# A second Strassen-Winograd level on one block product of seven, row statistics from sums, and a new emission order

## The chip, the cores and the metric

The kernel runs on one core of a Trainium2 chip, in fp32 throughout. The metric is the device time of one launch in microseconds, as the median over repeated runs. Besides the runs there is one execution recorded by the hardware profiler. Its rows name TensorE as PE (with PEld for its weight loads), VectorE as DVE, ScalarE as ACT, GpSimd as POOL and SyncE, which issues most DMAs, as SP.

## The reference

The input `x` is 128 batch entries of 128 nodes by 512 features, `adj` a 128 by 128 matrix. Four layers follow, each `x = layernorm(x + layer(x))` over the 512 features:

```
layer 0:  (adj x) W0 + bias
layer 1:  q = x Wq^T, k = x Wk^T, v = x Wv^T; rel = adj^T * (q k^T), each row divided by its norm; rel v
layer 2:  h = x W; s1, s2 = h a1, h a2; e = leaky_relu(s1 + s2^T) * adj; elu(softmax(e) h + beta h)
layer 3:  max over nodes of relu(...), with adj as both weights
```

The kernel uses that layer 1's `q k^T` is `(x M) x^T` with `M = Wq^T Wk`, that layer 2's `softmax(e) h + beta h` is `((softmax(e) + beta I) x) W`, and that layer 3's maximum collapses to `relu(max(adj x) + b)`, one value per row, which is added to the row of `x`.

## The kernel before

**Tiling.** Four batch entries form a group, and there are 32 groups (`G = 4`, `NG = 32`). A group passes through four products of 512 by 512 by 512: `y` (layer 0, times `W0`), `m` (layer 1, times `M`), `v` (layer 1, times `Wv`) and `z` (layer 2, times `W`). Around them stand smaller TensorE pieces for each batch entry: aggregates `p_y` (`adj x`, transposed), scores `p_rel`, attends `p_o`, gathers `p_z` and widens `p_a` (layer 3).

**One product.** `product` (L350) does each of the four with one Strassen-Winograd level: seven block products of 256 by 256 by 256 in place of eight. One block product is four matmuls with 256 moving columns (`by_rows` L324, `by_columns` L337). In the profile an fp32 matmul is two instructions, so a block product is a row of eight. The left factors are sums of blocks of the transposed activations, made on GpSimd (`left_factors` L305). The right factors are sums of weight blocks, made once on VectorE (`weight_blocks` L157). The block products run in the order 1, 2, 6, 5, 7, 3, 4. They are accumulated in three PSUM regions: products 1, 6, 7 and 4 in one bank (tag `r0`, two buffers), and product 2, then 5 and 3, in another (tag `r12`, one buffer). After each product the region is read out (`out`, L380), by a ScalarE copy or a VectorE add, and the next product into that region has to wait for this read.

**PSUM.** The eight banks are `r0` twice, `r12` once, `wa` (two banks that hold constant rows for the dots) and three of tag `ps` (`bank`, L85), which all the smaller pieces take in turn.

**Statistics.** Every layernorm takes `bn_stats` and `bn_aggr` on VectorE (`stats`, L397), a small VectorE operation and a power on GpSimd (`spread` in `norm`, L408), a small VectorE operation (`shift`) and an apply per batch entry on ScalarE. In layer 1, `residual` (L590) makes the new row on VectorE and takes its statistics directly after it, and `dots` (L605) follows with two multiply-and-sum operations per entry. In layer 2, `exp` on ScalarE and `elu` (L807) on VectorE do the same for its output. Layer 3 takes its own sums: squares on ScalarE, a maximum on VectorE and, on ScalarE, an add of that maximum that also sums the row (`top`, L860). Its `spread` (L868) works on these sums.

**Order.** Each engine executes in program order, and the order of the program is written by hand. Every piece is emitted at a time from `TABLE` (L235), in units of which a group takes 28. `FIRST` and `LAST` override it for the first two and the last three groups. All pieces of all groups are sorted by their time, so that in one period of 28 units four groups are interleaved: `m` of one group, `y` of the next, `v` of the first again, `z` of the group before. A piece emits its instructions on all engines it uses at one point: an aggregate, for instance, is four matmuls and the ScalarE copy behind them. Transposes of `x` for layer 1, of `rel` and of `e` are made in 32 by 32 blocks on VectorE (`turn_blocks`, `turn_rel`, `turn_blocks_2`) and completed by DMAs from the SP queue (`move`, `move_rel`, `move_2`); so is the spreading of `s2`, which `leaky` (L690) reads. Groups 0 and 1 use TensorE transposes (`turn`, L500), as do the softmax weights of the last two groups (`turn_att`, L734).

Of the kernel before, what the change touches and what calls it, by code (L numbers as in the profile page):

```python
# [8 lines left out]
FP = mybir.dt.float32  # L9
# [4 lines left out]
EPS = 1e-5  # L14
# [15 lines left out]
def kernel(  # L30
# [54 lines left out]
    def bank(name):  # L85
        return psum.tile([P, D], FP, tag="ps", name=name, bufs=3)

# [31 lines left out]
    nc.sync.dma_start(w2_sb, w2.rearrange("(k p) f -> p k f", p=P))  # L119
    a_sb = data.tile([P, 2, D], FP, tag="x3", name="a_sb")  # L120
    nc.sync.dma_start(a_sb.rearrange("p s d -> p (s d)"), on_all(a2, 2 * D))
# [35 lines left out]
    def weight_blocks(at, key, w, keep=0, tag=None):  # L157

        def blk(kh, ch):
            return w[:, 2 * kh : 2 * kh + 2, H * ch : H * ch + H]

        t = {}

        def factor(i):
            if i == 0:
                home, args = (const, {}) if tag is None else (data, dict(tag=tag))
                u = home.tile([P, 3 + keep, 2, H], FP, name=f"t_{key}", **args)
                t.update({2: u[:, 0], 3: u[:, 1], 4: u[:, 2]})  # L170
                t[1] = u[:, 3] if keep else blk(0, 1)
                bw[key] = {
                    1: blk(0, 0), 2: blk(1, 0), 3: blk(1, 1), 4: t[4], 5: t[1], 6: t[2], 7: t[3],
                }
            to, left, op, right = (
                (3, blk(1, 1), ALU.subtract, blk(0, 1)),
                (2, t[3], ALU.add, blk(0, 0)),
                (4, blk(1, 0), ALU.subtract, t[2]),
                (1, blk(0, 1), ALU.subtract, blk(0, 0)),
            )[i]  # L180
            dve.tensor_tensor(t[to], left, right, op)

        for i in range(4):
            emit(at[i], factor, i)

    bw = {}

# [9 lines left out]
    def prepare_dots(k):  # L197

        for i in range(2):
            scr = work.tile([P, D], FP, tag="scr", name=f"scr_wa_{i}_{k}", bufs=2)  # L200
            dve.scalar_tensor_tensor(
                scr,
                w2_sb[:, k, :],
                1.0,
                a_sb[:, i, :],
                op0=ALU.mult,
                op1=ALU.mult,
                accum_out=col[:, i, k : k + 1],
            )
# [21 lines left out]
    def row(at, step, n=G):  # L231
        return [at + i * step for i in range(n)]


    TABLE = dict(  # L235
        load=[-20], y=row(0.5, 1), y_sums=row(4.3, 0.5), y_w=row(7, 1, 7),
        stats0=row(14.4, 0.4), norm0=[16.2], apply0=row(16.8, 0.33),
        turn=row(21.4, 1), turn_blocks=row(18.4, 0.6),
        move=row(20.5, 0.1), x_sums=row(25.3, 0.5), m=row(28, 1, 7), scores=row(36.5, 1),
        masked=[39.95], squares=[40.4], turn_rel=[40.3],  # L240
        move_rel=row(41.2, 0.1), inverse=[42.5], v=row(42, 1, 7), attend=row(50.6, 1),
        residual=row(51.0, 1), dots=[51.7, 53.8, 54.9, 55.6], norm1=[54.6], scale=[57.2],
        apply1=row(65.4, 0.33),
        spread=[57.3], leaky=[62.6], weighted=[62.9], greatest=[63.9], exps=[64.0],
        divide=[65.2], turn_att=[68.6], with_beta=[69.0], turn_blocks_2=[65.7], move_2=[65.8], gather=row(71.5, 1),
        z_sums=row(75.3, 0.5), z_w=row(77, 1, 7), exp=[86.0, 87.0, 96.0, 99.6],
        elu=[86.4, 87.4, 96.8, 100.3], norm2=[101.4], apply2=row(102.4, 0.33),
        widen=[104.2, 104.9, 105.6, 106.3], top=[104.7, 105.4, 106.1, 106.8],
        norm3=[107.4], apply3=row(108.4, 0.33), store=[109.8],
    )  # L250

    FIRST = {
        0: dict(stats0=row(15.8, 0.02), norm0=[15.95], apply0=row(18.0, 0.1), turn=row(20.4, 0.3),
                dots=row(57.8, 0.1), scale=[58.9], spread=[61.6]),
        1: dict(y=row(-9.5, 0.3), y_sums=row(-4.0, 0.1), apply0=row(18.0, 0.1), turn=row(20.3, 0.3),
                x_sums=row(22.5, 0.5)),
# [47 lines left out]

    def left_factors(at, s, aT, tag, name, keep):  # L305

# [14 lines left out]
        emit(at[2], lambda: pool.tensor_tensor(s["f"][7], blk(0, 0), blk(1, 0), ALU.subtract))  # L321
        emit(at[3], lambda: pool.tensor_tensor(s["f"][3], blk(0, 1), s["f"][6], ALU.subtract))

    def by_rows(p, a, b, first):  # L324
# [24 lines left out]

    def product(at, name, mul, s, w, c, fresh, begin=None, before=None, lead=0.7):  # L350

# [28 lines left out]
        def out(i):  # L380
# [3 lines left out]
            else:  # L384
                dve.tensor_tensor(dst, p, dst, ALU.add)

        for n, i in enumerate(ORDER):
            if before is not None and i in (1, 5):
                emit(at[n] - (0.7 if i == 5 else lead), fill, REGION[i])
            emit(at[n], step, i)  # L390
            emit(at[n] + 0.72, out, i)
# [11 lines left out]

    def norm(at, apply_at, s, g, t):

        n = G // len(at)

        def spread(i):  # L408
            sl = slice(i * n, i * n + n)
            ve = small.tile([P, n], FP, tag=f"ve{n}", name=f"ve_{g}_{i}")  # L410
            dve.tensor_scalar(ve, s["mv"][:, sl, 1], EPS, None, op0=ALU.add)
            s["r", i] = small.tile([P, n], FP, tag=f"rstd{n}", name=f"rstd_{g}_{i}")
            pool.tensor_tensor(s["r", i], ve, mhalf[:, sl], ALU.pow)
# [24 lines left out]
    def layer0(g, t):  # L438
        s = {}

        def aggregate(b):
# [13 lines left out]
            )  # L455

        if g > 0:
            emit(t["load"][0], load, g)
        each(t["y"], aggregate)
        left_factors(t["y_sums"], s, "yT", "s_yz", f"y_{g}", 0)  # L460
        product(
# [7 lines left out]
            before=bias_halves,  # L469
            lead=4.4 if g == 0 else 0.7,  # L470
        )
        each(t["stats0"], lambda b: stats(s, f"0_{g}", b, x1[g][:, b, :]))
# [3 lines left out]
    def layer1(g, t):  # L476
        s = {}


# [110 lines left out]
        def residual(b):  # L590
            if b == 0:
                x2[g] = data.tile([P, G, D], FP, tag="x2", name=f"x2_{g}")
            dve.scalar_tensor_tensor(
                x2[g][:, b, :],
                s["o", b],
                s["rn"][:, b : b + 1],
                x1[g][:, b, :],
                op0=ALU.mult,
                op1=ALU.add,
            )  # L600
            if g < NG - 1:
                stats(s, f"1_{g}", b, x2[g][:, b, :])


        def dots(b):  # L605
            if b == 0:
                s["d"] = small.tile([P, 2, G], FP, tag="d12", name=f"d12_{g}")
            for i in range(2):
                scr = work.tile([P, D], FP, tag="scr", name=f"scr_{g}_{b}_{i}", bufs=2)
                dve.scalar_tensor_tensor(  # L610
# [26 lines left out]
        else:  # L637
            each(t["turn_blocks"], turn_blocks)
            each(t["move"], move)
        left_factors(t["x_sums"], s, "xT", "s_x", f"x_{g}", 1)  # L640
        product(t["m"], f"m_{g}", by_columns, s, "m", middle_block, True, begin_middle)
        each(t["scores"], scores)
# [7 lines left out]
        emit(t["inverse"][0], inverse)  # L650
        product(t["v"], f"v_{g}", by_rows, s, "v", rows_of(lambda: s["v"]), True, begin_values)
        each(t["attend"], attend)
# [4 lines left out]
        emit(t["scale"][0], scale_dots)  # L657
        norm(t["norm1"], t["apply1"], s, f"1_{g}", lambda: x2[g])

# [5 lines left out]
    def layer2(g, t):  # L665
        s = {}
        late = g >= NG - 2


# [64 lines left out]
        def turn_att(i):  # L734
            if i == 0:
                s["p"] = bank(f"p_eT_{g}")
            for b in range(i * n, i * n + n):
                pe.transpose(s["p"][:, b * P : (b + 1) * P], s["e"][:, b, :], ident)

        def with_beta(i):  # L740
            if i == 0:
                s["eT"] = work.tile([P, G, P], FP, tag="eT", name=f"eT_{g}")
            dve.tensor_tensor(
                s["eT"][:, i * n : i * n + n, :],
                s["p"].rearrange("p (b n) -> p b n", b=G)[:, i * n : i * n + n, :],
                beta_b[:, i * n : i * n + n, :],
# [60 lines left out]
        def elu(b):  # L807
            if b == 0:
                if g < NG - 1:
                    x3[g] = data.tile([P, G, D], FP, tag="x3", name=f"x3_{g}")  # L810
                else:
                    x3[g] = work.tile([P, G, D], FP, tag="xB", name=f"x3_{g}")
# [3 lines left out]
            )  # L816
            dve.scalar_tensor_tensor(x, s["m", b], 1.0, x, op0=ALU.min, op1=ALU.add)
            stats(s, f"2_{g}", b, x)

# [14 lines left out]
        if g < NG - 1:  # L834
            left_factors(t["z_sums"], s, "zT", "s_yz", f"z_{g}", 0)
            product(t["z_w"], f"z_{g}", by_rows, s, "2", rows_of(lambda: s["c"]), True, begin)
        else:
            each(t["z_w"], direct)
        each(t["exp"], exp)
        each(t["elu"], elu)  # L840
        norm(t["norm2"], t["apply2"], s, f"2_{g}", lambda: x3[g])

    def layer3(g, t):
        s = {}

        def widen(b):
            s["a", b] = bank(f"p_a_{g}_{b}")
            pe.matmul(s["a", b], adjT, x3[g][:, b, :], start=True, stop=True)  # L850
# [155 lines left out]
```

## Time and profile before

| What | Value |
|---|---|
| time, median of 3 runs | 2174.16 us (2173.9 to 2174.24) |
| the profiled execution, its time | 2173.83 us |
| its span, first to last instruction | 2172.0 us |
| mean granted TensorE clock | 0.996 |
| TensorE busy | 2149.1 us, 99% |
| VectorE busy | 1560.6 us, 72% |
| ScalarE busy | 1115.4 us, 51% |
| GpSimd busy | 720.8 us, 33% |
| DMA queue of SP | 135.22 MB, 24.8% of 16 engines |

Busy time is the time in which an engine had an instruction in it. TensorE's instructions overlap, so its pace is read from the starts of consecutive instructions and not from their durations. The span is what the rows cover; the execution's time is 1.83 us longer. "Idle before" in a row is what the engine stood still ahead of that group, with the releaser behind an arrow. Line L26 stands in nearly all rows, because one helper records every instruction; the names of the tiles tell the rows apart.

### The profile page before, as it was taken

What the parts mean: (1) busy time and instruction counts of PE and PEld (TensorE: products, weight loads), DVE (VectorE), ACT (ScalarE), POOL (GpSimd) and SP (SyncE); (2) the same over time, 40 slices, a digit from 0 to 9 for tenths busy, and PEclk for the clock granted to TensorE, in tenths of its full rate; (3) what the DMA queues carried; (4) which work ended last, traced back from release to release, by engine and by line L of the source; (5) the groups of instructions that cost most, each with busy time, mean ns of one, the idle gap of its engine ahead of it and who ended that gap; (6) DMA issues with size and microseconds to landing.
All of it is one profiled execution on the core that took longest, in us unless ns stands there. A gap on an engine that the chain in (4) does not pass through costs nothing.

```text
span 2172.0 us, 31973 instructions
## 1 busy us (share of the span) xinstructions
PE 2149.1 (99%) x10887; PEld 1820.3 (84%) x10887; DVE 1560.6 (72%) x3429; ACT 1115.4 (51%) x2470; POOL 720.8 (33%) x589
## 2 busy tenths in 40 slices
PE   9999999999999999999999999999999999999996
PEld 8888888888888888888888888888888888888882
DVE  4667676776777776777777767767777767777677
ACT  3235545555545555455555455554455554555554
POOL 4223333333333233334233233323332333333331
PEclk9999999999999999999999999999999999999998
DMA  4012222322122322222222223222322222332201
GB/s 171 25 37 64 58 72 72 71 54 59 59 76 66 77 55 51 67 73 69 55 58 62 74 71 73 54 56 62 75 67 66 58 56 70 74 68 55 39 20 59
DMA packets 361970, 138.31 MB, mean 64 GB/s; under 512 B 303184, under 2 KB 318672, under 8 KB 361808
## 3 DMA queue, kind: packets, MB, share of 16 engines
q1 hardware_dynamic: 361280, 135.22, 24.8%
q8 instruction: 88, 1.44, 0.3%
q10 hardware_dynamic: 528, 1.05, 0.1%
q14 instruction: 74, 0.61, 0.1%
HBM read 55.12 MB, written 41.48 MB: 44 GB/s over the span
## 4 chain that ended last, share of the span: by engine, by line
PE 97%; DVE 2%; ACT 0%; POOL 0%; issue 0%; ACTq 0%; POOLq 0%; DVEq 0%
PE r_m L26 18%; PE r_y L26 18%; PE r_v L26 18%; PE r_z L26 17%; PE p_rel L26 5%; PE p_y L26 5%; PE p_o L26 5%; PE p_z L26 5%; PE p_a L26 5%; PE r_qk L26 1%; DVE st L26 1%; DVE x L26 0%; DVE mx L26 0%; PE first_r L26 0%; ACT x L26 0%; PE c L26 0%
## 5 line engine op out<-in xcount | busy, mean ns | idle before, releaser
L26 ACT ACTIVATE x<-x,nmean,rstd 128x512 f32<-128x512 f32 x384 | 285.4, 807 | 48.6 <-DVE nmean L26 45.1
L26 DVE BATCH_NORM_STATS2 st<-x 128x6 f32<-128x512 f32 x392 | 268.3, 685 | 9.7 <-ACT x L26 1.1
L26 POOL TENSOR_TENSOR rstd<-ve,mhalf 128x4 f32<-128x4 f32 (+1 forms) x99 | 109.3, 1104 | 340.3 <-DVE ve L26 340.3
L26 DVE TENSOR_TENSOR x<-r_y,x 128x512 f32<-128x512 f32 x224 | 152.4, 680 | 91.7 <-PE r_y L26 83.7
L26 ACT COPY yT<-p_y 128x512 f32<-128x512 f32 x128 | 74.9, 586 | 195.6 <-PE p_y L26 195.6
L26 DVE SCALAR_TENSOR_TENSOR scr<-x,wa 128x512 f32<-128x512 f32 x256 | 162.0, 679 | 0.0
L26 DVE TENSOR_REDUCE mx<-p_a 128x1 f32<-128x512 f32 x128 | 88.3, 690 | 99.6 <-PE p_a L26 96.8
L26 ACT ACTIVATE x<-x,mean,r 128x512 f32<-128x512 f32 x128 | 97.4, 808 | 113.9 <-DVE mean L26 112.4
L26 POOL TENSOR_TENSOR rn<-n,mhalf 128x4 f32<-128x4 f32 x32 | 32.6, 1017 | 358.3 <-ACT sq L26 358.3
L26 PEld LDWEIGHTS p_z<-eT,x 128*128 128x128 f32 x1024 | 133.8, 192 | 8.0 <-issue 0.9
L26 PEld LDWEIGHTS p_rel<-xT,tT 128*128 128x128 f32 x1024 | 134.0, 192 | 6.7 <-ACT tT L26 0.2
L26 PEld LDWEIGHTS p_y<-adjT,x 128*128 128x128 f32 x1024 | 133.6, 192 | 6.3
L26 ACT COPY tT<-r_m 128x512 f32<-128x512 f32 x128 | 75.6, 590 | 119.1 <-PE r_m L26 119.1
L26 DVE TENSOR_TENSOR tT<-r_m,tT 128x512 f32<-128x512 f32 x96 | 66.3, 691 | 96.9 <-PE r_m L26 94.2
L26 PE MATMUL p_rel<-xT,tT 128*128 128x128 f32 x1024 | 134.7, 275 | 0.0
L26 PE MATMUL p_z<-eT,x 128*128 128x128 f32 x1024 | 134.5, 275 | 0.1
L26 PE MATMUL p_y<-adjT,x 128*128 128x128 f32 x1024 | 134.1, 275 | 0.0
L26 POOL TENSOR_TENSOR s_y<-yT 128x512 f32<-128x512 f32 x32 | 40.6, 1269 | 281.1 <-ACT yT L26 281.1
L26 PE MATMUL p_a<-x,adjT 128*128 128x512 f32 x256 | 128.7, 606 | 5.1 <-ACT x L26 5.1
L26 ACT COPY zT<-p_z 128x512 f32<-128x512 f32 x128 | 73.7, 576 | 116.5 <-PE p_z L26 116.5
L26 PE MATMUL p_o<-v,relT 128*128 128x512 f32 x256 | 129.7, 592 | 0.0
L26 ACT COPY v<-r_v 128x512 f32<-128x512 f32 x128 | 74.2, 580 | 107.9 <-PE r_v L26 107.9
(157 smaller groups left out, 5218.7 us busy)
## 6 DMA issues: line engine op xcount, KB each, us to landing
out_dram<-x SPq DMA_DIRECT2D x128, 256.0 KB, 2.1
x<-in_x_dram SPq DMA_DIRECT2D x31, 1024.0 KB, 7.6
xT<-xB SPq DMA_DIRECT2D x480, 64.0 KB, 2.3
relT<-relB SPq DMA_DIRECT2D x496, 16.0 KB, 1.8
eBd<-eB SPq DMA_DIRECT2D x30, 256.0 KB, 2.0
eT<-eBd SPq DMA_DIRECT2D x120, 64.0 KB, 2.0
s<-s2d SPq DMA_DIRECT2D x29, 256.0 KB, 5.2
w_sb<-in_L_gnn_weight_dram ACTq DMA_DIRECT2D x1, 1024.0 KB, 6.0
```

Source lines behind the costliest of these rows:

```text
L26: return lambda *args, **kw: self.tc.keep_in_program_order(op(*args, **kw))
```

## The change

Block product 2 is itself split by Strassen-Winograd into seven products of 128 by 128 by 128 (`inner_product`). It is done so for `y` in groups 2 to 31, `m` and `v` in groups 1 to 30, and `z` in groups 0 to 29. The seven run in four steps between the other six block products, in a bank of their own (tag `pi`, one buffer), for which `ps` gives up one of its three. After each step VectorE adds one or two 128-column slots into the destination; there are seven such adds per product in place of one 512-column add. Four sums on GpSimd for each set of left factors (`inner_sums`; `m` and `v` share one set) and four on VectorE for each weight matrix, once, make the factors.

The statistics of layer 1 (groups 0 to 30) and layer 2 (groups 0 to 28) come from sums: `residual` and `elu` also accumulate the row sum, and ScalarE squares the row with a sum (`square`). `norm` gets three more small VectorE operations for it.

`TABLE` has new times for nearly every piece: aggregates, scores and gathers stand in pairs, the leaky pair stands ahead of the `out` of block product 3 of `m`, and the exponentials ahead of `m`'s first copy. `EARLY` keeps old times for groups 0 and, in part, 1. The buffers of `x3` and of the dots' scratch go from two to one. In the last groups some transposes and widens use the `pi` and `r12` banks.

```diff
     def bank(name):
-        return psum.tile([P, D], FP, tag="ps", name=name, bufs=3)
+        return psum.tile([P, D], FP, tag="ps", name=name, bufs=2)
...
+        def inner_sums():
...
+            pool.tensor_tensor(s1, a[1, 0], a[1, 1], ALU.add)
+            pool.tensor_tensor(s2, s1, a[0, 0], ALU.subtract)
+            pool.tensor_tensor(s3, a[0, 0], a[1, 0], ALU.subtract)
+            pool.tensor_tensor(s4, a[0, 1], s2, ALU.subtract)
+            s["fi"] = {1: a[0, 0], 2: a[0, 1], 3: s4, 4: a[1, 1], 5: s1, 6: s2, 7: s3}
+
+        if inner:
+            emit(at[2] + inner, inner_sums)
...
+    SMALL = (
+        ((1, 2), (((0, 0), 1), ((0, 0), 0))),
+        ((6, 5), (((1, 1), 2), ((0, 1), 0))),
+        ((7,), (((1, 1), 0),)),
+        ((4, 3), (((0, 1), 2), ((1, 0), 0))),
+    )
...
+    STEPS = {
+        key: (
+            {1: (0.0, 0.45), 6: (1.69, 2.4), 5: (2.62, 3.3), 7: (4.22, 4.9), 3: (5.16, 5.85), 4: (5.91, 6.6)},
+            ((1.5, 1.65), (2.43, 2.6), (4.12, 4.18), (4.97, 5.15)),
+        )
+        for key in ("m", "0", "v")
+    }
...
+        def step(n):
+            if n == 0:
+                q["p"] = psum.tile([P, Q, P], FP, tag="pi", name=f"pi_{name}", bufs=1)
+            for i in SMALL[n][0]:
+                a, b = s["fi"][i], bw_inner[w][i]
+                pe.matmul(
+                    q["p"][:, {2: 1, 5: 2, 3: 2}.get(i, 0), :],
+                    b if columns else a,
+                    a if columns else b,
+                    start=(i == 1),
...
+        def out(n):
+            for (j, h), i in SMALL[n][1]:
...
+                dve.tensor_tensor(dst, q["p"][:, i, :], dst, ALU.add)
...
+    def square(s, g, b, x):
+        scr = work.tile([P, D], FP, tag="scr3", name=f"scr3_{g}_{b}")
+        act.activation(scr, x, AF.Square, accum_out=s["sq"][:, b : b + 1])
...
+            if from_sums:
...
+                dve.tensor_scalar(m, s["add"], 1.0 / D, None, op0=ALU.mult)
+                dve.tensor_scalar(
+                    s["sq"], s["sq"], 1.0 / D, EPS, op0=ALU.mult, op1=ALU.add
+                )
+                dve.scalar_tensor_tensor(ve, m, -1.0, m, op0=ALU.mult, op1=ALU.mult)
+                dve.tensor_tensor(ve, ve, s["sq"], ALU.add)
...
-            if g < NG - 1:
-                stats(s, f"1_{g}", b, x2[g][:, b, :])
+                **(dict(accum_out=s["add"][:, b : b + 1]) if summed else {}),
+            )
...
-                scr = work.tile([P, D], FP, tag="scr", name=f"scr_{g}_{b}_{i}", bufs=2)
+                scr = work.tile([P, D], FP, tag="scr", name=f"scr_{g}_{b}_{i}")
...
-                    x3[g] = data.tile([P, G, D], FP, tag="x3", name=f"x3_{g}")
+                if g < NG - 2:
+                    x3[g] = data.tile([P, G, D], FP, tag="x3", name=f"x3_{g}", bufs=1)
...
-        masked=[39.95], squares=[40.4], turn_rel=[40.3],
+        masked=[38.85], squares=[39.2], turn_rel=[39.1],
...
-        spread=[57.3], leaky=[62.6], weighted=[62.9], greatest=[63.9], exps=[64.0],
+        spread=[57.3], leaky=[61.3], weighted=[62.6], greatest=[63.2], exps=[63.25],
```

## The prediction

> **What bounds the kernel now.** I read the page first, then the stretches by stage, TensorE's own waits, TensorE's instructions in order of time and the groups by shape.
>
> ```profile
> PE 2149.1 (99%) x10887; PEld 1820.3 (84%) x10887; DVE 1560.6 (72%) x3429; ACT 1115.4 (51%) x2470; POOL 720.8 (33%) x589
> ...
> PE 97%; DVE 2%; ACT 0%; POOL 0%; issue 0%; ACTq 0%; POOLq 0%; DVEq 0%
> ```
>
> TensorE holds 97% of the chain that ended last. Busy is not yet "without a hole", so three stretches follow (length, then PE, PEld, DVE, ACT, POOL busy):
>
> ```profile
> 0.00:66.00 66.00, 64.05 (x341) 54.88 (x342) 33.83 (x62) 19.37 (x33) 22.89 (x23) 1.00 0.39 141
> 1012.46:1078.43 65.97, 65.97 (x337) 56.28 (x336) 47.61 (x104) 34.98 (x78) 22.21 (x18) 1.00 0.27 64
> 2068.00:2172.00 104.00, 83.24 (x354) 57.50 (x352) 76.72 (x201) 53.19 (x110) 21.49 (x23) 0.93 0.08 32
> ```
>
> The middle line is one whole group period, from one m product's start to the next: 65.97 us, all of it TensorE, at clock 1.00. VectorE has 18 us free there, ScalarE 31, GpSimd 44. Only the first 66 us (2 us idle) and the last 104 us (21 us idle) have holes. TensorE's waits agree: the longest is in the tail.
>
> ```profile
> PE p_a L26 <- ACT x L26: 5.1, 3, 3.2
> ...
> PE r_z L26 <- POOL s_z L26: 0.9, 1, 0.9
> ```
>
> So a microsecond less of TensorE work per period is a microsecond of time, as long as no new wait opens.
>
> **What is removed and added on TensorE.** Its timeline gives the true pace, start to start (the printed durations overlap):
>
> ```profile
> 1012.46 1.89 PE L26 MATMUL r_m<-xT,m_qk 128*128 128x256 f32 x8
> 1014.19 1.05 PE L26 MATMUL p_y<-adjT,x 128*128 128x128 f32 x8
> 1015.08 1.89 PE L26 MATMUL r_m<-xT,m_qk 128*128 128x256 f32 x8
> 1016.81 1.05 PE L26 MATMUL p_y<-adjT,x 128*128 128x128 f32 x8
> ```
>
> Eight 256-wide instructions (four fp32 matmuls, one block product) take 1.73 us, 0.216 each. Eight 128-wide ones (four matmuls, each with its own weights) take 0.89 us, 0.112 each, also between wider ones. Block product 2 (4 matmuls of 256) becomes seven of 128: 8 x 0.216 = 1.73 against 14 x 0.112 = 1.57, so 0.16 us less.
>
> Here a rule speaks against the change. The Trainium skill, TensorE: Matmul & The Clock Gate, Back-to-back issue gap, says that in a stream of load-and-multiply pairs both operations set the pace, and gives 81 ns at 128 columns and 131 at 512. On a line between them 256 costs 98 ns, an estimate from that page. Then 14 x 81 - 8 x 98 is +0.35 us per product, 42 us slower in all. This trace's 112 against 216 is nearly in proportion to width, with a fresh weight load each time. The measurement decides.
>
> How many products: m and v for groups 1 to 30, y for 2 to 31, z for 0 to 29: 4 x 30 = 120. 120 x 0.16 = 19.3 us. The period falls from 65.97 to 65.33.
>
> **The other engines' work, per period.** The rows for it:
>
> ```profile
> L26 DVE BATCH_NORM_STATS2 st<-x 128x6 f32<-128x512 f32 x392 | 268.3, 685 | 9.7 <-ACT x L26 1.1
> L26 DVE BATCH_NORM_AGGREGATE mv<-st 128x2 f32<-128x6 f32 x392 | 71.3, 182 | 13.5
> L26 DVE TENSOR_TENSOR v<-r_v,v 128x512 f32<-128x512 f32 x96 | 65.7, 685 | 52.5 <-PE r_v L26 27.2 <-ACT v L26 25.3
> L26 DVE TENSOR_TENSOR eT<-p_eT,beta_i 128x128 f32<-128x128 f32 x4 | 1.2, 291 | 1.5 <-PE p_eT L26 1.4
> L26 ACT ACTIVATE scr<-x 128x512 f32<-128x512 f32 x120 | 74.3, 620 | 0.1
> L26 POOL TENSOR_TENSOR s_y<-yT 128x512 f32<-128x512 f32 x32 | 40.6, 1269 | 281.1 <-ACT yT L26 281.1
> ```
>
> VectorE gains 4 x 7 small adds from PSUM, 28 x 0.291 = 8.1 us, eight accumulator reads at 0.081 (the dots' row) and six small statistics operations at 0.16: +9.8. It loses four 128x512 adds (2.7) and eight bn_stats with bn_aggr (8 x 0.867 = 6.9): -9.7. It stays at 47.7 of 65.3. ScalarE gains eight squares, 8 x (0.620 + 0.190) = 6.5: 41.5. GpSimd gains three lots of four 128x128 adds; no row has that shape: 0.32 us if the 1.27 row shrinks with size, 1.27 if not at all. I take 0.35 (fixed cost looks small at 512 columns), 4 us; at 1.27 it is 15 us, and GpSimd is still under 38. No engine overtakes TensorE; the question is order.
>
> **The new wait.** Each inner step adds into a slot that VectorE must first have read, so between two inner steps TensorE waits for two small adds. All later TensorE work queues behind that wait. The tightest gaps hold one block product, 1.73 us; the adds need some 0.2 to start and 0.5 to run: 1.0 us to spare. One 0.69 us operation in flight fits; VectorE standing in a wait of its own does not. I walked the queues in the new order, phases from the start of m:
> - m step 1: TensorE would start it at 5.7. VectorE has ended the old group's dots at 65.9 and its small sums near 67.9 of the period before (2.6 here), idles, reads at 4.2 to 4.7. Spare 1.0. Steps of y and v: the same 1.0.
> - scores (17.2) now stand behind m's third add, since the leaky pair was put ahead of it on VectorE. Those two cost what the next lines show, 1.30 + 1.60 beside GpSimd's sums, against 0.69 for such operations alone. The s2 broadcast lands near 9 (d at 67.9, plus the 6.7 us it took before), so the pair starts at 13.0, after the step 3 reads, and ends at 15.9; the add ends at 16.6. Spare 0.6.
> - v: four bn_stats pairs stand ahead of its first reads, but end (35.1) as those are due. n0's shift after them waits 1.1 us for GpSimd's power, and n2's sums for ScalarE's last square (39.0 to 40.2); the v reads behind each are wanted 2 and 1 us later.
> - z step 2 (57.8): VectorE first needs layer 3's sums, which wait for ScalarE's last "x plus top". ScalarE ended that 2.3 us after the last widen before; widen now ends at 51.7, so 54.0 to 54.4. Then 0.7 of small operations, 0.65 residual, 0.5 reads: 56.2. Spare 1.5.
>
> ```profile
> 1093.21 1.30 DVE L26 TENSOR_TENSOR e<-s,d 128x512 f32<-128x512 f32 x1
> 1093.61 1.98 POOL L26 TENSOR_TENSOR s_y<-yT,s_y 128x512 f32<-128x512 f32 x1
> ...
> 1094.54 1.60 DVE L26 SCALAR_TENSOR_TENSOR e<-e 128x512 f32<-128x512 f32 x1
> ```
>
> So every inner step costs nothing beyond its matmuls, covered by at least 0.6 us; if a cover goes, the excess times 30 is the price.
>
> **One bank and one x3 buffer fewer.** Two "ps" banks instead of three. In the steady period the tightest are the third and fourth attend, which need residuals 0 and 1: 55.7 against 59.7, 58.8 against 60.6. Widen 2 needs maximum 0: 48.3 against 50.0. Aggregate 2 needs ScalarE's copy of aggregate 0: 3.4 against 7.9; scores and gathers, now also in pairs, stand alike. Free. x3 is rewritten at 70 (4.7 of the next period), its stores ended 2.5 us after the last apply before, so near 65.1 with applies until 62.6: 4.9 us to spare. One scr buffer could cost VectorE 0.1 per dot, 0.8 per period, in idle time.
>
> **Moved steps.** Transposes to xB go 1.5 us earlier, with their 16 xT DMAs; SP's order (s2, load, eB and eT, relT, xT, stores) is unchanged, so nothing new stands ahead of them. On GpSimd e's mask now stands ahead of y's inner sums and fourth sum: it leaves near 17.2, so the inner sums end near 18.6 and y step 1 wants them at 21.2; all x sums precede n1's power, free because n1's apply comes far later.
>
> **The ends.** Four transposes of x with eight PSUM uses at the start took 4.2 us for 3.6 of TensorE work with three banks; with two I put +0.8 (0.3 to 1.5), group 1's turns +0.4, the first attends in a row +0.15. In the tail, attends in a row wait for residuals: +0.3 (-1 to +1, as the pi and r12 banks also serve there). The 16 one-time weight sums (16 x 0.29 = 4.7 us of VectorE) lie where VectorE idles: 0. Sum +1.6.
>
> **Sum.** The profiled execution took 2173.83 (span 2172.0 and 1.8 around it), 0.3 under the median of 2174.16. 2173.83 - 19.3 + 1.6 = 2156.1; on the median 2156.5.
>
> **The rivals.**
> 1. Full gain, no steady stall: 2156.5; with the ends' bounds 2152 to 2162. For it: spare of 0.6 or more at every wait, and an old period without a hole. Against: spares from one hand-walked period. 0.74.
> 2. Part of the gain goes: one spare was 0.3 us too large (say the leaky pair ahead of scores, or the single scr), 0.3 x 30 = 9 us back: 2166, between 2162 and 2170. 0.12.
> 3. Slower. ScalarE, with 6.5 us more per period, is late with layer 3's "x plus top" ahead of z step 2: the order has VectorE hold residual 0 and the reads until that sum is in. Price: the lateness beyond 55.9, each period. It decides from 56.5 (2.1 us later than I find: 0.59 us x 30 = 17.7, the whole net gain). At 57 the stall is 1.1 x 30 = 33, so 2190. For: ScalarE rises to 64% busy and carries four squares just there. Against: those four stood there before too, and the new ones fall later or earlier. 0.10.
> 4. The inner level saves nothing, because weight loads of short runs do not hide as between p_y and r_m: 2175.8, within no change. The timeline speaks against it. 0.04.
>
> **How the numbers follow.** About 0.2% (4.3 us) is what a measurement of this kernel can tell from no change. Faster than 2169.8: all of case 1, most of case 2: 0.85. Within: 0.06, case 4 and the edges of 2 and 3. Slower: 0.09. The range 2152 to 2168 holds case 1 and most of 2 and leaves out under two in ten.
>
> **What would show it.** Right: a period near 65.3 us with TensorE busy throughout, 960 instructions fewer in the r rows, 1680 in new pi rows at a pace of 0.112; bn_stats down by some 240; VectorE near 48 and ScalarE near 41 per period. Wrong: TensorE idle before pi or before p_rel, released by VectorE, in every period (case 2, 3), or a pi pace well above 0.112 (case 4); idle growing past 2 us in the first 130 us or past 21 in the last 104 (my ends).

## The result: 2155.26 us, and the profile after

| | before | after |
|---|---|---|
| time, median | 2174.2 us (4 runs on the same chip) | 2155.26 us (4 runs, 2154.96 to 2155.7) |
| ratio after to before | | 0.9913, 95% interval 0.9896 to 0.993 |
| span of the profiled execution | 2172.0 us | 2153.9 us |

Predicted were 2156.5 us and a range of 2152 to 2168. The first part of the page (busy time, share, instructions) and its chain of work:

```profile
PE 2127.1 (99%) x11607; PEld 1827.1 (85%) x11607; DVE 1492.6 (69%) x4105; ACT 1283.9 (60%) x2950; POOL 862.9 (40%) x949
...
PE 96%; DVE 2%; ACT 1%; SPq 0%; POOL 0%; issue 0%; DMA 0%; ACTq 0%; POOLq 0%; DVEq 0%
```

TensorE has 720 instructions more (1680 new less 960 old) and is busy for 22 us less. It still holds the chain. The three stretches of the prediction, in the profile after (length, then PE, PEld, DVE, ACT, POOL busy, clock, DMA):

```profile
0.00:66.00 66.00, 63.33 (x330) 53.51 (x331) 38.09 (x69) 19.56 (x33) 22.19 (x23) 1.00 0.40 141
1004.83:1070.11 65.28, 65.28 (x361) 56.55 (x360) 45.76 (x128) 40.52 (x94) 27.74 (x32) 1.00 0.27 65
2049.90:2153.90 104.00, 80.69 (x347) 55.90 (x345) 74.16 (x195) 52.81 (x110) 20.24 (x22) 0.94 0.08 31
```

The middle one is again a whole period: 65.28 us for the predicted 65.33. The first has 2.7 us of idle TensorE (before 1.95), the last 23.3 (before 20.8). TensorE's timeline around the inner steps of `m` (start, duration, engine, line, operation, count):

```profile
1006.56 1.95 PE L26 MATMUL p_y<-adjT,x 128*128 128x128 f32 x16
1008.34 0.61 PE L26 MATMUL pi_m<-xT,m_qk 128*128 128x128 f32 x4
1008.79 1.89 PE L26 MATMUL r_m<-s_x,t_m 128*128 128x256 f32 x8
1010.52 0.61 PE L26 MATMUL pi_m<-si_x,u_m 128*128 128x128 f32 x4
1010.96 1.89 PE L26 MATMUL r_m<-s_x,m_qk 128*128 128x256 f32 x8
```

Four new instructions take 0.445 us from start to start, 0.111 each (predicted 0.112), and no row has idle time in brackets. TensorE's waits show only single ones, at the start and in the tail; no `pi` wait repeats by period:

```profile
PE p_a L26 <- ACT x L26: 6.2, 4, 3.2
...
PE r_z L26 <- DVE c L26: 1.1, 1, 1.1
PE r_z L26 <- POOL s_z L26: 0.6, 1, 0.6
PE pi_m L26 <- DVE tT L26: 0.6, 1, 0.6
```

**Where the 18.1 us of span came from.** Reading the starts of `m`'s first block product in both timelines splits the span into four stretches (prediction: its own terms, sorted into them):

| stretch | before | after | difference | predicted |
|---|---|---|---|---|
| start to group 2's m | 153.77 | 155.38 | +1.61 | +0.7 |
| group 2's m to group 3's | 65.93 | 66.09 | +0.16 | -0.6 |
| 28 periods, to group 31's m | 1849.34 | 1827.84 | -21.50 | -18.0 |
| group 31's m to the end | 102.96 | 104.59 | +1.63 | +0.3 |
| sum | 2172.00 | 2153.90 | -18.10 | -17.6 |

The sum is met; two of its terms are not. The 28 periods gave 3.5 us more than forecast, and the other three stretches took 3.0 more. The experiments ask for the cause of each.

### The profile page after: what moved, and what is told of

Same layout as the page of the kernel before. It is cut to its first block, busy times and chain, and to the rows that moved or that the text cites. A ratio compares the mean times of both kernels' runs of the same rounds, so it can differ in the third digit from the quotient of the medians.

```text
span 2153.9 us, 34894 instructions
## 1 busy us (share of the span) xinstructions
PE 2127.1 (99%) x11607; PEld 1827.1 (85%) x11607; DVE 1492.6 (69%) x4105; ACT 1283.9 (60%) x2950; POOL 862.9 (40%) x949
## 4 chain that ended last, share of the span: by engine, by line
PE 96%; DVE 2%; ACT 1%; SPq 0%; POOL 0%; issue 0%; DMA 0%; ACTq 0%; POOLq 0%; DVEq 0%
PE r_y L26 16%; PE r_v L26 16%; PE r_m L26 15%; PE r_z L26 14%; PE p_rel L26 5%; PE p_y L26 5%; PE p_z L26 5%; PE p_o L26 5%; PE p_a L26 5%; PE pi_v L26 2%; PE pi_y L26 2%; PE pi_m L26 2%; PE pi_z L26 2%; DVE st L26 1%; SPq L26 0%; ACT x L26 0%
## 5 line engine op out<-in xcount | busy, mean ns | idle before, releaser
L26 ACT ACTIVATE scr<-x 128x512 f32<-128x512 f32 x360 | 226.1, 628 | 147.6 <-DVE x L26 142.5
L26 POOL TENSOR_TENSOR rstd<-ve,mhalf 128x4 f32<-128x4 f32 (+1 forms) x99 | 99.1, 1001 | 390.3 <-DVE ve L26 390.0
L26 DVE TENSOR_TENSOR x<-r_y,x 128x512 f32<-128x512 f32 x194 | 132.5, 683 | 77.2 <-PE r_y L26 72.4
L26 DVE SCALAR_TENSOR_TENSOR scr<-x,wa 128x512 f32<-128x512 f32 x256 | 174.4, 681 | 4.6
L26 POOL TENSOR_TENSOR s_x<-xT 128x512 f32<-128x512 f32 x64 | 81.8, 1278 | 128.0 <-DMA xT<-xB 83.1
L26 PEld LDWEIGHTS p_y<-adjT,x 128*128 128x128 f32 x1024 | 124.1, 192 | 3.8 <-ACT yT L26 0.7
L26 PE MATMUL p_rel<-xT,tT 128*128 128x128 f32 x1024 | 125.1, 275 | 0.0
L26 ACT COPY c<-r_z 128x512 f32<-128x512 f32 x124 | 71.3, 576 | 86.6 <-PE r_z L26 86.6
L26 PE MATMUL r_y<-w_sb,s_y 128*128 128x256 f32 x512 | 121.1, 379 | 0.0
L26 PE MATMUL r_v<-t_v,s_x 128*128 128x256 f32 x512 | 121.1, 379 | 0.0
```

The lines of the kernel that those rows point to most:

```text
L26: return lambda *args, **kw: self.tc.keep_in_program_order(op(*args, **kw))
```

## The experiments

All medians are of 4 to 18 runs, and ratios are to before on the same chip. With 4 runs the intervals reach 3 to 4 us to either side, so the steps of about 1 us in experiments 5 and 6 are not shown by the medians alone; they rest on waits and periods in the traces. The theory at the outset: the seven-product level brings the time, the statistics and the order only make room. Its rivals: the new order or the sums bring part of it by themselves, and the level sits close to a wait that the prediction mis-measured.

**1. The level alone taken out.** Everything else of the change stays.

```diff
-        inner = g >= 2
+        inner = False
...
-        inner = 1 <= g < NG - 1
+        inner = False
...
-                inner=not late,
+                inner=False,
```

> The changed kernel with block product 2 whole again, everywhere: no inner products and no sums for them; statistics from sums, new order and two ps banks stay. Theory (TensorE sets the period, and the inner level's 0.16 us per product is the gain): TensorE's work per period goes back from 65.28 to 65.93, so 28 to 30 periods give back 0.65 each, 19.6 in all: 2175, no faster than the kernel before. Its period should be near 65.93 and still without the 0.11 us hole of before, so 2175 is made of before's 2174, 3.3 less for the hole and about 4 more for the ends. Rival (order and statistics make the gain, the inner level is a wash): near 2155 to 2160.

2175.74 us, ratio 1.0006 (0.9997 to 1.0014): 20.5 us above the changed kernel. Two neighbouring starts of `m` give its period, 65.93:

```profile
1015.02 1.89 PE L26 MATMUL r_m<-xT,m_qk 128*128 128x256 f32 x8
...
1080.95 1.89 PE L26 MATMUL r_m<-xT,m_qk 128*128 128x256 f32 x8
```

So the level takes 65.93 - 65.28 = 0.65 us from a period, 0.163 per product, and 120 x 0.163 = 19.6 in all (predicted 19.3). The rest of the 20.5 lies outside the full periods: this run waits once, in its start, for a late `d` (1.6 us ahead of `p_s`), and does not have the 0.8 of experiment 6. But before has the same TensorE work in 1849.34 / 28 = 66.05 us per period. The new order took 0.12 out of a period that the prediction called full.

**2. The hole of before.** Before's timeline of all engines near the end of `z`, of which the rows of the chain are kept:

```profile
1073.51 0.81 ACT L26 ACTIVATE x<-x,mean,r 128x512 f32<-128x512 f32 x1 [3.81 <-DVE mean L26]
...
1074.08 1.02 PE L26 MATMUL p_o<-v,relT 128*128 128x512 f32 x2
...
1074.23 0.56 ACT L26 COPY c<-r_z 128x512 f32<-128x512 f32 x1
...
1074.94 1.96 PE L26 MATMUL r_z<-w_sb,s_z 128*128 128x256 f32 x8
...
1076.74 1.89 PE L26 MATMUL r_z<-t,zT 128*128 128x256 f32 x8
```

Product 3 of `z` (1074.94) must wait for ScalarE's copy of product 5 out of the same region. That copy is queued behind the first apply of layer 3, which itself waits 3.81 us for a mean. It ends at 1074.79, product 3 starts 0.15 later, and its eight instructions need 1.80 us to the next start instead of 1.73. The row carries no idle bracket because the printed durations overlap (1.89 printed for 1.73). In before's 28 full periods, starts that come over 0.03 us late stand at this product in 20 of them, 3.2 us in all, and at no other place. To test it, before's applies are put just behind that copy:

```diff
-        norm3=[107.4], apply3=row(108.4, 0.33), store=[109.8],
+        norm3=[107.4], apply3=row(108.85, 0.33), store=[109.95],
```

> The kernel before with one edit: layer 3's applies on ScalarE 0.45 units later, so that z's copy of block product 5 stands ahead of the first of them. Theory: before's mean period of 66.04 against 65.93 of TensorE work is a hole of 0.11 us ahead of z's block product 3, which waits for that copy, queued behind an apply that waits for VectorE; it closes, period 65.93, 29 x 0.11 = 3.2 us faster: 2171. Rival (the 0.11 is TensorE's own pace between differently shaped groups): no change, 2174.

2170.63 us, ratio 0.9981 (0.9974 to 0.9988): 4.0 less by one moved time, and the period of before becomes even:

```profile
1011.41 1.89 PE L26 MATMUL r_m<-xT,m_qk 128*128 128x256 f32 x8
...
1077.35 1.89 PE L26 MATMUL r_m<-xT,m_qk 128*128 128x256 f32 x8
...
1143.28 1.89 PE L26 MATMUL r_m<-xT,m_qk 128*128 128x256 f32 x8
```

The hole is shown: the 28 periods take 1846.13 us here instead of 1849.34, 3.2 less. The remaining 0.8 of the median is in no period of the trace and lies within the interval (2.6 to 5.7 us faster). In the changed kernel this copy stands ahead of the applies too, so the gain is part of its result and none of its level's.

**3. bn_stats back.** The level stays, the row sums of layers 1 and 2 go.

```diff
-        summed = g < NG - 1
+        summed = False
...
-                **(dict(accum_out=s["add"][:, b : b + 1]) if summed else {}),
+            )
+            if g < NG - 1:
+                stats(s, f"1_{g}", b, x2[g][:, b, :])
...
-        summed = g < NG - 3
+        summed = False
```

> The changed kernel with bn_stats and bn_aggr again for layers 1 and 2 (no row sums, no extra squares on ScalarE); inner products, order and banks stay. VectorE gets back 6.9 us per period less 1.6 for sums and small operations, from 45.8 to about 51 of 65.3. Theory (spare at the waits of 0.6 to 1.5 us): most places hold, the place where the old group's last dots, its norm and the first m step meet is used up, since the shift of d waits for GpSimd's power later: 0 to 0.3 us per period, 2155 to 2165. Rival (statistics from sums are what makes the inner level fit): VectorE falls behind in z, over 0.65 us per period, 2175 or more.

2179.32 us, ratio 1.0021 (1.0014 to 1.0029). This theory's expectation was wrong and the rival's right: with the level and in this order, the sums are worth 24 us. VectorE is busy for 50.2 of a period of 66.04 us, still 16 free. What costs is where it stands when an inner step is due (timeline of all engines):

```profile
1080.38 0.69 DVE L26 BATCH_NORM_STATS2 st<-x 128x6 f32<-128x512 f32 x1
...
1084.85 0.17 DVE L26 TENSOR_SCALAR ve<-mv 128x4 f32<-128x4 f32 x1
...
1084.99 1.89 PE L26 MATMUL r_m<-s_x,t_m 128*128 128x256 f32 x8
1085.09 1.06 POOL L26 TENSOR_TENSOR rstd<-ve,mhalf 128x4 f32<-128x4 f32 x1 [2.59 <-DVE ve L26]
...
1086.19 0.17 DVE L26 TENSOR_TENSOR d<-d,rstd 128x8 f32<-128x8 f32 x1 [0.92 <-POOL rstd L26]
1086.27 0.61 DVE L26 TENSOR_TENSOR tT<-pi_m,tT 128x128 f32<-128x128 f32 x2
...
1087.03 0.68 PE L26 MATMUL pi_m<-si_x,u_m 128*128 128x128 f32 x4
```

In VectorE's order `ve` stands behind the last statistics (from 1080.38) and the dots that follow them; GpSimd's power waits 2.59 us for `ve`, VectorE stands 0.92 us for the power, and the reads are behind that. The product at 1084.99 has 1.73 us of work; the step behind it starts after 2.04, so 0.31 is lost there, and 0.07 more in the step's own first instructions. Two steps of `v` lose 0.26 and 0.10, which with 0.38 makes 0.74 of the 0.76 us that the period is longer. That the place of the statistics does it, and not their length, is read from these rows; no run put them elsewhere in the order. These are the places of the level with one block product between steps, as the prediction named them.

**4. Rival 3's price.** ScalarE's squares of layer 3, ahead of its last "x plus top", are issued twice for entries 2 and 3 (two squares more), then three times (four more), with the same result.

```diff
-            act.activation(scr, x3[g][:, b, :], AF.Square, accum_out=s["sq"][:, b : b + 1])
+            for _ in range(2 if b >= 2 else 1):
+                act.activation(scr, x3[g][:, b, :], AF.Square, accum_out=s["sq"][:, b : b + 1])
```

> The changed kernel with layer 3's squares of entries 2 and 3 done twice on ScalarE, in groups 0 to 29 (the result is the same): two operations of 0.71 us more ahead of the last x plus top, which VectorE waits for before residual 0 and the reads of z's inner step 1. Theory (the slower case of the prediction, as a queue): in the changed kernel the reads ended at 1061.13 and inner step 2 started at 1062.55, 1.4 us of spare; 0.2 of the added 1.4 falls into ScalarE's idle time, so 1.2 of the spare goes and nothing of the time: 2155 to 2157. Rival (the queue is not that tight, or ScalarE's work has more idle time to fall into): also no change; the next run tells.

> The same with those squares done three times: four operations, 2.8 us more, 2.6 after the idle time. Theory: 2.6 - 1.4 = 1.2 us late at z's inner step 2 in each of some 29 periods, 35 us slower than the changed kernel: 2190, with TensorE waiting for VectorE ahead of pi_z. Rival (lateness is caught up on the way, as VectorE and the attends have other work to put in between): less than 10 us slower, 2155 to 2165.

2165.06 us, ratio 0.9956 (0.9941 to 0.9971), and 2208.8 us, ratio 1.0158 (1.0143 to 1.0174). The chain of one period in the first of the two: ScalarE's end of "x plus top", the reads of `z` step 1, and the start of step 2.

```profile
1064.62 0.19 ACT L26 ACTIVATION_READ_ACCUMULATOR x<-x,top 128x1 f32 x1
...
1066.27 0.48 DVE L26 TENSOR_TENSOR c<-pi_z,c 128x128 f32<-128x128 f32 x2
...
1066.90 0.46 PE L26 MATMUL pi_z<-u,si_z 128*128 128x128 f32 x2
```

With two squares more the period is 65.60, 0.32 longer, where the theory expected none; with four it is 67.11, and the time 19 us above the expected 2190. In the changed kernel the reads end at 1061.13 and step 2 starts at 1062.55, so 1.42 us seemed spare. Here the reads end at 1066.75 and the step starts 0.15 later: that hand-over from VectorE's end to TensorE's start is not spare, and 1.27 remain. Two squares cost 1.5 us (0.75 each, one behind the other into one scratch tile): 1.5 - 1.27 = 0.23 of the 0.32. Another 0.07 is the step itself, whose two instructions take 0.29 us to the next start after a stall and 0.22 otherwise. The next two cost 67.11 - 65.60 = 1.51 per period, their full length. The second expectation was low for the same reasons: a square costs 0.75 and not 0.71, none of it fell into idle time, and the hand-over and the slower step were not counted. So past the threshold ScalarE's lateness is paid one to one, in every period.

**5. The ends.** First, the third bank back where the ends lost time: the `pi` bank serves single uses of the smaller pieces in groups 0, 1, 30 and 31, in which it is free.

```diff
-    def bank(name):
+    def bank(name, third=False):
+        if third:
+            return psum.tile([P, D], FP, tag="pi", name=name, bufs=1)
...
-        pv = bank(f"p_wv{c}")
+        pv = bank(f"p_wv{c}", c in (0, 2))
...
-            s["o", b] = bank(f"p_o1_{g}_{b}")
+            s["o", b] = bank(f"p_o1_{g}_{b}", (g, b) in ((0, 1), (NG - 1, 2)))
```

> The changed kernel in which the pi bank serves as third bank where it is idle: weight transposes 0 and 2, group 1's aggregate 2 and turn 2, group 0's attend 1, the last group's attend 2 and group 30's gather 1. Theory: the bank is what the start lost (0.30 + 0.24 + 0.32 + 0.19 + 0.24 + 0.37 of waits, 0.32 of them there before) and a third of what the tail lost (0.48): 1.3 + 0.5 = 1.8 us faster than the changed kernel, 2153.5. Rival (the start is longer because of VectorE's and ScalarE's new work, or by chance): no change from 2155.3.

2154.0 us, ratio 0.9906 (0.9892 to 0.9919). The waits of aggregates, transposes and attends in the start that before did not have are gone, and group 0's `m` starts at 44.3 instead of 46.4 (before: 44.4), but a wait of 1.3 has come in:

```profile
PE r_m L26 <- DVE tT L26: 1.3, 1, 1.3
```

Second, two scratch tiles for the last group's dots, on top of it. The changed kernel's tail, timeline of all engines:

```profile
2087.40 0.69 DVE L26 SCALAR_TENSOR_TENSOR scr<-x,wa 128x512 f32<-128x512 f32 x1
...
2088.13 0.69 DVE L26 SCALAR_TENSOR_TENSOR scr<-x,wa 128x512 f32<-128x512 f32 x1
...
2092.85 0.68 DVE L26 TENSOR_TENSOR c<-r_z,c 128x512 f32<-128x512 f32 x1
...
2093.59 1.99 PE L26 MATMUL r_z<-t,s_z 128*128 128x256 f32 x8 [1.09 <-DVE c L26]
```

With one scratch tile the dots start 0.73 us apart; before, with two, 0.60 (2106.70 and 2107.30). Eight of them make the add behind them a microsecond late, and TensorE waits for it.

```diff
-                scr = work.tile([P, D], FP, tag="scr", name=f"scr_{g}_{b}_{i}")
+                scr = work.tile([P, D], FP, tag="s2" if (g, i) == (NG - 1, 1) else "scr", name=f"scr_{g}_{b}_{i}")
```

> The run with the third bank at both ends, and the last group's second dots write to another scratch (an idle buffer), so that successive dots no longer write the same one. Theory: in the tail the eight dots went from 0.61 to 0.73 us apart, which is the 1.1 us that z's block product 5 of group 30 waits for VectorE; with two scratches this wait goes: 1.0 us faster than with the bank alone, 2153.0. Rival (the dots' pace has another cause, such as the bank that they read): no change, 2154.0.

2152.74 us, ratio 0.99 (0.9883 to 0.9916). The 1.09 wait is gone: all sixteen instructions run in a row.

```profile
2089.54 3.85 PE L26 MATMUL r_z<-t,s_z 128*128 128x256 f32 x16 [0.90 <-POOL s_z L26]
```

Third, the wait of 1.3. In that version VectorE, just ahead of group 0's first read of `m`, makes the four one-time sums that the inner level needs of `M`:

```profile
45.36 1.61 POOL L26 TENSOR_TENSOR s_x<-xT 128x512 f32<-128x512 f32 x1
45.76 1.35 DVE L26 TENSOR_TENSOR u_m<-m_qk 128x128 f32<-128x128 f32 x1
...
49.65 1.34 DVE L26 TENSOR_TENSOR u_m<-m_qk 128x128 f32<-128x128 f32 x1
...
50.92 0.68 DVE L26 TENSOR_TENSOR tT<-r_m,tT 128x512 f32<-128x512 f32 x1
...
51.65 1.99 PE L26 MATMUL r_m<-s_x,m_qk 128*128 128x256 f32 x8 [1.29 <-DVE tT L26]
```

The four run from 45.76 to 51.00, 1.24 to 1.35 us each beside GpSimd's sums of `x`. The prediction put them at 0.29 each and none on the path. No group needs them before group 1.

```diff
-            emit(at[3], inner)
+            emit(41.0 if key == "m" else at[3], inner)
```

> The version with the third bank at the ends and the second scratch, and the four one-time sums of blocks of M for the inner level (u_m) emitted 12 units later. Theory: these four took 1.3 us each instead of the 0.29 that the prediction put (they share the window with GpSimd's sums), stand on VectorE ahead of group 0's first read of m, and make the 1.29 us wait of TensorE at 51.65. Moved, group 0's third block product starts 1.3 earlier, and the whole is 2152.74 - 1.3 = 2151.4, the 65.28 period unchanged. Rival: the read is late for another reason (the four t_m sums ahead of it, 42.9 to 45.8), or group 1 waits for something later in the start anyway: then no gain, 2152.7.

2151.93 us, ratio 0.9897 (0.9881 to 0.9914): the wait is gone, and group 0's `m` to group 1's takes 46.07 us instead of 47.62. In the median 0.8 of the expected 1.3 shows; the four runs spread over 1.2 us.

**6. Group 2's late step.** The table above has group 2's period at 66.09 and not 65.28. The changed kernel's timeline of all engines there:

```profile
153.09 1.27 POOL L26 TENSOR_TENSOR s_x<-xT 128x512 f32<-128x512 f32 x1 [10.84 <-DMA xT<-xB]
...
156.03 0.94 DVE L26 TENSOR_SCALAR mean<-add 128x4 f32<-128x4 f32 x1
...
157.01 1.19 DVE L26 SCALAR_TENSOR_TENSOR ve<-mean 128x4 f32<-128x4 f32 x1
...
159.91 1.02 POOL L26 TENSOR_TENSOR rstd<-ve,mhalf 128x4 f32<-128x4 f32 x1
160.96 0.17 DVE L26 TENSOR_TENSOR d<-d,rstd 128x8 f32<-128x8 f32 x1 [1.82 <-POOL rstd L26]
161.05 0.61 DVE L26 TENSOR_TENSOR tT<-pi_m,tT 128x128 f32<-128x128 f32 x2
...
161.81 0.68 PE L26 MATMUL pi_m<-si_x,u_m 128*128 128x128 f32 x4 [0.58 <-DVE tT L26]
```

GpSimd's eight sums for group 2 wait for the transfers of `xT`, the power of group 1's norm is queued behind them, VectorE stands 1.82 us for it, and the reads behind VectorE are late. A first attempt moved only what follows the product with `rstd`:

```diff
-                x_sums=row(22.5, 0.5)),
+                x_sums=row(22.5, 0.5), spread=[57.75]),
```

> The same, and group 1's spread (VectorE's product d<-d,rstd) put behind the first inner step's two reads of group 2's m. Theory: at that place VectorE stands 1.8 us for GpSimd's power, which stands behind group 2's four sums and four inner sums, which waited for the xT transfers; the reads queued behind it are late, and TensorE waits 0.56 and starts the step about 0.7 late. Behind the reads it costs nothing: 0.7 to 0.8 less than the run without it, 2150.6 to 2150.7, and the period of group 2 is 65.28 like the others. Rival: other small operations of VectorE stretched beside GpSimd's sums (mean 0.93, ve 1.18) make the reads late by themselves: then under 0.3 less.

2151.56 us, ratio 0.9895 (0.988 to 0.991). No step moved, so the 0.4 us between the medians is scatter: the product is emitted by `scale` and not by `spread`, so VectorE's order was the old one and the 1.82 stayed. It says nothing on the theory. The second attempt moved `scale` with it:

```diff
-                x_sums=row(22.5, 0.5)),
+                x_sums=row(22.5, 0.5), scale=[57.7], spread=[57.75]),
```

> The version with the weight sums late (third bank at the ends, second scratch, u_m later), and group 1's three operations on d (the two products with wa_sum and the one with rstd) put behind the first two reads of group 2's m; in the run before only the transfers behind them had moved, and VectorE kept its order. Theory: VectorE's 1.82 us stand for GpSimd's power is what makes TensorE wait 0.5 and start the inner step 0.65 to 0.7 late (the start of group 2's m to the step's start is 6.32 to 6.38 there, against 5.68 in later groups). Behind the reads it costs nothing: the step starts at 5.7, group 2's period is 65.28 like the others, and the time 2151.93 - 0.7 = 2151.2. Rival: the small operations ahead (mean 0.9, ve 1.2, beside GpSimd's sums) are late by themselves, or the later leaky pair makes another wait: step at 5.9 or later, or period over 65.6; under 0.3 less.

2150.7 us, ratio 0.9891 (0.9875 to 0.9908), 1.2 below the version without it. The trace shows 0.7 of that, in group 2's period; the rest is about as large as the scatter just seen. The reads now wait for TensorE and not TensorE for them, and its next step starts 5.69 us after `m`'s start as in later groups (timeline of all engines). Group 3's `m` starts at 218.62, so group 2's period is 65.28 (65.99 in the version without it):

```profile
153.34 1.89 PE L26 MATMUL r_m<-xT,m_qk 128*128 128x256 f32 x8
...
157.57 0.62 DVE L26 TENSOR_TENSOR tT<-pi_m,tT 128x128 f32<-128x128 f32 x2 [0.99 <-PE pi_m L26]
157.88 1.02 POOL L26 TENSOR_TENSOR rstd<-ve,mhalf 128x4 f32<-128x4 f32 x1
...
158.94 0.17 DVE L26 TENSOR_TENSOR d<-d,rstd 128x8 f32<-128x8 f32 x1 [0.49 <-POOL rstd L26]
...
159.03 0.61 PE L26 MATMUL pi_m<-si_x,u_m 128*128 128x128 f32 x4
```

The small operations are slow here too (mean 0.95, ve 1.19 us), so the rival that blamed those falls. This version is the fastest: 23.5 us under before, 4.6 under the change as made, about what the ends had cost.

## Why the prediction was right, and where it was not

- **The level's saving: right.** 0.111 us per new instruction against 0.112, 0.163 per product against 0.16, 19.6 against 19.3. From the rates in the Trainium skill, TensorE: Matmul & The Clock Gate, Back-to-back issue gap, the prediction had estimated that the level would be 42 us slower; run 1 decides for the trace's proportion to width.
- **"An old period without a hole": wrong by 0.12 us per period.** The step that failed is reading 65.97 us busy out of 65.97 as a period without a hole. An instruction's printed end lies about 0.16 us behind its pace (1.89 against 1.73 for eight), so a late start of 0.07 leaves no gap. The window also ended 0.03 short: that period is 66.00, and in before's trace the full periods go from 65.93 to 66.27, 66.05 in the mean, so one window could not show it. Run 2 showed the hole and its cause, worth 3.2 us, which the prediction had in no term.
- **The spares: right in the main.** Measured in the changed kernel against predicted: `m` step 1 0.84 against 1.0, the leaky pair from 12.9 to 15.8 against 13.0 to 15.9, scores at 17.2 with the add ended at 16.4 against 16.6, `z` reads ended at 56.3 against 56.2. What the walk left out is the hand-over of 0.15 us between VectorE's end and TensorE's start, by which the spare at `z` was too large. Busy time per period came to 45.8 us on VectorE (47.7 put), 40.5 on ScalarE (41.5) and 27.7 on GpSimd (26.2).
- **Rival 3: right in mechanism and price, its onset too late.** A lateness was to be paid from 1.5 us on and is paid from 1.27. With 3.0 us more of ScalarE's work the kernel was slower than before, as that rival has it; as made it keeps clear of it.
- **bn_stats: a load without a place.** The prediction set the statistics' VectorE time against free time (-9.7 against +9.8). Run 3's rows put the loss down to their place ahead of the dots: with them the period is longer with the level (66.04) than without it (65.93, run 2), with 16 us of VectorE free.
- **The ends: +1.6 put, about +4.7 paid** (the three stretches of the table outside the 28 periods, with the level's 0.65 taken out of the first two). The prediction's own sign for this came: TensorE is idle for 2.9 us of the first 130 (2 was the limit) and for 23.3 of the last 104 (21). The parts:
  - The banks. Up to group 0's `m` +0.8 was put and 1.4 paid (33.5 us against 32.1 from the first product of `y`); for group 1's turns and the first attends +0.55 was put and 0.6 paid (46.71 against 46.07 from group 0's `m` to group 1's). The first version of experiment 5 takes both away, and 0.5 us in the tail.
  - Another 0.6 of the start lies ahead of the first product of `y`. It varies between runs of the same start and is not the change's for all that is known. A wait of 0.3 that before had in the start is gone.
  - The single scratch, called "in idle time": true in the steady period, but 1.2 us in the tail, where VectorE is what TensorE waits for (group 31's `m` to the end took 104.1 us without and 102.9 with the second scratch).
  - The weight sums, called 0 at 0.29 each: three of the four took 1.3 to 1.4. As the change was made they cost nothing, because the banks had already made the start late; with the banks put right they cost 1.3.
  - Group 2's period, 0.8, was in no term. The step that failed was the walk in phases of one steady period, where the power is early enough.

The two wrong sizes, -3.2 for the hole and +3.1 for the ends, have nothing to do with each other and cancel. So it is luck that the total was met to 0.06%; the total alone would have hidden both.

## What to carry to other kernels

A bottleneck engine that is busy in every slice can still lose time in each period: compare starts between consecutive rows, and whole periods with each other, before calling it full. In an in-order queue, a step's spare is what its readers have left after every instruction ahead of them, hand-over included; free time of the engine elsewhere buys nothing. A buffer given up has to be priced apart in the first and last groups: here the bank and the scratch cost nothing in the steady period, in which no start comes late, and about 3.7 us at the ends, and a wait removed there uncovered the next.

## What the hardware showed that was not expected

- VectorE operations of next to no data stretch beside GpSimd's sums. In the rows of experiment 6 `mean`, on four columns, took 0.94 us and `ve` 1.19, where such an operation takes 0.16 alone (prediction); each ended within 0.03 us of the end of a GpSimd sum. Of the four sums of `M`'s blocks in the changed kernel, the first found GpSimd idle and took 0.28 us; the others ran beside 512-column sums and took about as long as one of these (1.27). The first two:

```profile
46.45 0.28 DVE L26 TENSOR_TENSOR u_m<-m_qk 128x128 f32<-128x128 f32 x1
46.76 1.27 POOL L26 TENSOR_TENSOR s_x<-xT 128x512 f32<-128x512 f32 x1 [0.78 <-ACT xT L26]
46.76 1.41 DVE L26 TENSOR_TENSOR u_m<-u_m,m_qk 128x128 f32<-128x128 f32 x1
```

The Trainium skill, SBUF — State Buffer, Who interferes with whom, says that VectorE and GpSimd share a pair of ports, and that a VectorE operation with two inputs in SBUF contends with a GpSimd operation that reads SBUF. The block sums and `ve` have two inputs and agree. `mean` has one, so this sentence does not cover it, and what held it is not shown.

- GpSimd's 128x128 add takes 0.46 us (459 ns over 60 of them), more than a quarter of the 1.27 for 512 columns (0.32) and far less than all of it. The prediction took 0.35.
